# Dense passes of a four-layer graph network as one stream of steps, with layer 2 begun inside the graph norm

## The chip, the cores and the metric

The kernel runs on one core of a Trainium2 chip. TensorE (PE), VectorE (DVE), ScalarE (ACT) and GpSimd (POOL) each work through a queue of their own in order; SyncE (SP) issues most of the DMAs. Tensors live in HBM, tiles in SBUF, matmul results in PSUM. The metric is device time in microseconds (us); lower is better. A kernel is timed in several runs, and one further execution is profiled.

## What is computed

The graph has 6250 nodes with 128 features, and 206250 directed edges sorted by target. Four layers follow each other, each on `h = relu(layernorm(x))`. The reference, cut to what matters (edges as `src`, `dst`):

```python
# layer 0
nb = segment_sum(edge_weight[:, None] * h[src], dst)
x += leaky_relu(nb @ W1.T + b1 + (h * nb) @ W2.T + b2, 0.2)
# layer 1: mean over neighbours, then a norm over all nodes of the graph
f = gelu((segment_sum(h[src], dst) / max(deg, 1)) @ Wl.T + bl + h @ Wr.T)
out = f - mean_scale * mean(f)
x += out / sqrt(mean(out * out) + EPS) * gn_weight + gn_bias + h
# layer 2: nodes take the mean of clique rows
x += (segment_sum(x_clique[dst], src) / max(count, 1)) @ W.T + b
# layer 3: one message pass and a GRU cell
hh = h @ W_in.T + b_in
agg = segment_sum((hh @ W_msg)[src], dst)
r, z, n = gates(agg @ W_ih.T + b_ih, hh @ W_hh.T + b_hh)
x += ((1 - z) * n + z * hh) @ W_out.T + b_out
```

In layer 2, indices of `x_clique` (3125 rows) above the last one read the last row.

## The kernel before

Nodes are cut into 49 blocks of 128 (`NB`). A first stage, up to about 1225 us, counts for every pair of blocks how many edges lead from node to node. It writes the counts to HBM in bf16 as `cnt_d`, and a transposed copy as `cntT_d`, and does layer 0 on the way. With the counts, every later `segment_sum` is a dense product: the counts times the rows of the layer's input. Those are the three dense passes, each made by one call of the generator `dense` (L838 to L872), for layer 1 with `h_parts`, layer 2 with `q_parts` (the clique rows, 25 blocks, `NQB`) and layer 3 with `m_parts`.

`dense` goes over 13 chunks of up to four blocks of output nodes (`CHUNKS`; the seventh has one block). For each chunk it fills one PSUM accumulator `acc` (two buffers) in steps: seven steps of seven blocks for layers 1 and 3 (`by_node`), five steps of five blocks for layer 2. A step

- loads its rows of counts from `cnt_d` (L847, 896 KB) or `cntT_d` (L852, 640 KB) into a `ring` tile (three buffers), by SP's queue;
- turns them from bf16 into fp32r, some blocks on DVE into `some` (L858) and the others on ACT into `others` (L859), two buffers each; in layer 1 the same is done block by block with a sum taken along (L865, L868), which gives the degrees of layer 2;
- multiplies, two matmuls for each block (L870), since each input is kept as two halves whose sum is the fp32 value.

After a chunk's last step `dense` yields, and the caller works on that chunk.

- Layer 1 (from L943): copy `acc` to `agg`, a product with `wl`, scale and add, Gelu, and a sum over nodes on POOL. The first chunk is taken earlier, at L883 (`first = next(layer1)`); after it in the source stand the loads of `f` from `f_d` (L886), weights, the degrees (L902), and the clique rows `xq` (L914 to L918).
- The graph norm (L957 to L988): the mean from the sums (`over_all`, L938), then for each of 13 groups of four blocks a subtraction of `center` on DVE (L979), a square on ACT (L981) and a sum on POOL (L929, L932), then the `gain`.
- Layer 2 (from L993): copy of `acc` (L997), product with `wc` (L1001), load of `x` from `u_d` (L1004; tile `x` has two buffers), bias on POOL (L1005), `f` times gain and added to `x` (L1006, L1007), the chunk's update (L1009, L1012), the layer norm (helper `norm`, L554 to L565), the next bias on POOL (L1017), the store to `x_d` (L1018), and the input of layer 3 (L1021 to L1033: `hh`, `msg` and its halves in `m_parts`).
- Layer 3 (from L1036): the GRU gates, and the result.

No order is written out by hand. The framework that builds the program plans each engine's order itself: of the instructions whose inputs and buffers are ready at its planned time, it takes the one that stands first in the source. It then adds the waits. So a queue need not follow the source: the loads L1004 of layer 2's first two chunks are issued at 1199.9 us, in the counting stage, and matmuls of layer 2 run before layer 1's last product L950 at 1560.6 us. On the chip each queue is then worked through in the planned order, whether or not the times come out as planned.

Of the kernel before, what the change touches and what calls it, by code (L numbers as in the profile page):

```python
# [9 lines left out]
F32 = mybir.dt.float32  # L10
I32 = mybir.dt.int32
BF16 = mybir.dt.bfloat16
AF = mybir.ActivationFunctionType
ALU = mybir.AluOpType
DVE = mybir.EngineType.DVE

P = 128
D = 128
N = 6250
NB = -(-N // P)  # L20
# [453 lines left out]
CB = 4  # L474
NQB = -(-NQ // P)
CHUNKS = [(g, min(CB, n - g)) for b, n in ((0, NQB), (NQB, NB)) for g in range(b, n, CB)]
NCH = len(CHUNKS)
CHUNK_OF = {g + j: (c, j) for c, (g, nb) in enumerate(CHUNKS) for j in range(nb)}
KB = 7
KQ = 5  # L480
NSMP = -(-E // P)
F32R = mybir.dt.float32r
# [3 lines left out]
def fast(ctx: ExitStack, tc: tile.TileContext, a: dict, out: bass.AP, flag: bass.AP):  # L486


    nc = tc.nc
# [35 lines left out]
    cnt_d = dram.tile([NCH, P, CB, NB * P], BF16, name="cnt_d")  # L525
    cntT_d = dram.tile([P, NQB, NPAD], BF16, name="cntT_d")
# [54 lines left out]
    with ExitStack() as bx:  # L581
# [4 lines left out]
        psum = bx.enter_context(tc.tile_pool(name="b_psum", bufs=1, space=bass.MemoryType.PSUM))  # L586
# [250 lines left out]

    def dense(parts, by_node, seen=None):  # L838

        last, step, dve = (NB, KB, 4) if by_node else (NQB, KQ, 3)  # L840
        for c, (g, nb) in enumerate(CHUNKS):
            w = nb * P
            acc = psum.tile([P, CB * P], F32, name="acc", bufs=2)
            for q in range(0, last, step):
                if by_node:
                    t = ring.tile([P, CB, KB, P], BF16, name="ring")
                    nc.sync.dma_start(t[:, :nb].rearrange("p b k n -> p b (k n)"),  # L847
                                      cnt_d[c, :, :nb, q * P : (q + KB) * P])
                    t = t[:, :nb].rearrange("p b k n -> p k b n")
                else:  # L850
                    t = ring.tile([P, KQ, CB, P], BF16, name="ring")
                    nc.sync.dma_start(t[:, :, :nb].rearrange("p k b n -> p k (b n)"),  # L852
                                      cntT_d[:, q : q + KQ, g * P : g * P + w])
                    t = t[:, :, :nb]
                some = wide.tile([P, 4, CB, P], F32R, name="some")
                others = wide.tile([P, 3, CB, P], F32R, name="others")
                if seen is None:
                    nc.vector.tensor_copy(some[:, :dve, :nb], t[:, :dve])  # L858
                    nc.scalar.copy(others[:, : step - dve, :nb], t[:, dve:])  # L859
                for i in range(step):  # L860
                    rhs = some[:, i, :nb] if i < dve else others[:, i - dve, :nb]
                    if seen is not None:
                        total = seen[:, c, q + i : q + i + 1]
                        if i < dve:
                            nc.vector.tensor_scalar(rhs, t[:, i], 1.0, None, op0=ALU.mult,  # L865
                                                    op1=ALU.add, accum_out=total)
                        else:
                            nc.scalar.activation(rhs, t[:, i], AF.Copy, accum_out=total)  # L868
                    for j in range(2):
                        nc.tensor.matmul(acc[:, :w], parts[:, q + i, j, :], rhs,  # L870
                                         start=q + i + j == 0, stop=q + i + j == last)
            yield g, nb, acc  # L872


    h_parts = late.tile([P, NB, 2, D], F32R, name="parts")
# [4 lines left out]
        halves(nc.vector, [h_parts[:, g : g + nb, i, :] for i in range(2)], f[:, g : g + nb, :])  # L880
    deg2 = late.tile([P, NCH, NB], F32, name="deg2")
    layer1 = dense(h_parts, True, deg2)
    first = next(layer1)  # L883

    for g, nb in GROUPS:
        nc.sync.dma_start(f[:, g : g + nb, :], rows(f_d, g, nb))  # L886
# [22 lines left out]
    for g in range(0, NQB, GB):  # L909
        nb = min(GB, NQB - g)  # L910
# [14 lines left out]
    def over_nodes(total, blocks, g, nb):  # L925

        full = nb if g + nb < NB else nb - 1
        if full:
            nc.gpsimd.tensor_tensor(total[:, :full, :], total[:, :full, :], blocks[:, :full, :], op=ALU.add)  # L929
        if full < nb:  # L930
            last = total[:NR, full, :]
            nc.gpsimd.tensor_tensor(last, last, blocks[:NR, full, :], op=ALU.add)  # L932

    def over_all(total):

        p = psum.tile([P, D], F32, name="pS")
        for j in range(CB):
            nc.tensor.matmul(p, ones, total[:, j, :], start=j == 0, stop=j == CB - 1)  # L938
        return p

    f_sum = late.tile([P, CB, D], F32, name="f_sum")
    nc.gpsimd.memset(f_sum, 0.0)
    for g, nb, acc in chain((first,), layer1):  # L943
        w = nb * P
        agg = work.tile([P, CB * P], F32, name="wa")
        nc.scalar.copy(agg[:, :w], acc[:, :w])
        pa = psum.tile([P, CB * D], F32, name="pA")
        for j in range(nb):
            s = slice(j * D, (j + 1) * D)
            nc.tensor.matmul(pa[:, s], agg[:, s], wl, start=True, stop=True)  # L950
        for j in range(nb):
            nc.vector.scalar_tensor_tensor(f[:, g + j, :], pa[:, j * D : (j + 1) * D],
                                           inv1[:, g + j : g + j + 1], f[:, g + j, :],
                                           op0=ALU.mult, op1=ALU.add)
        fg = flat(f[:, g : g + nb, :])
        nc.scalar.activation(fg, fg, AF.Gelu)
        over_nodes(f_sum, f[:, g : g + nb, :], g, nb)  # L957
    p_sum = over_all(f_sum)
    center = late.tile([P, D], F32, name="center")
    nc.vector.scalar_tensor_tensor(center, p_sum, 1.0 / N, mean_scale, op0=ALU.mult, op1=ALU.mult)  # L960
# [12 lines left out]
    nc.vector.tensor_reduce(to_last, by_source[:, :, -(-NQB // CB) :], axis=mybir.AxisListType.X, op=ALU.add)  # L973
    nc.vector.tensor_mul(to_last, to_last, inv2)

    sq_sum = late.tile([P, CB, D], F32, name="f_sum")
    nc.gpsimd.memset(sq_sum, 0.0)
    for g, nb in GROUPS:
        nc.vector.tensor_sub(f[:, g : g + nb, :], f[:, g : g + nb, :], bcast(center, nb))  # L979
        sq = work.tile([P, GB, D], F32, name="wb")  # L980
        nc.scalar.activation(sq[:, :nb, :], f[:, g : g + nb, :], AF.Square)  # L981
        over_nodes(sq_sum, sq, g, nb)
    p_sq = over_all(sq_sum)
    gain = late.tile([P, D], F32, name="gain")
    nc.vector.tensor_scalar(gain, p_sq, 1.0 / N, EPS, op0=ALU.mult, op1=ALU.add)
# [3 lines left out]


    m_parts = late.tile([P, NB, 2, D], F32R, name="parts")
    hh = fh
    for g, nb, acc in dense(q_parts, False):  # L993
        w = nb * P
        cols = slice(g * P, g * P + w)
        agg = work.tile([P, CB * P], F32, name="wa")
        nc.scalar.copy(agg[:, :w], acc[:, :w])  # L997
        pa = psum.tile([P, CB * D], F32, name="pA")
        for j in range(nb):
            s = slice(j * D, (j + 1) * D)  # L1000
            nc.tensor.matmul(pa[:, s], agg[:, s], wc, start=True, stop=True)  # L1001
        x = work.tile([P, CB, D], F32, name="x")
        xg, fg = x[:, :nb, :], f[:, g : g + nb, :]
        nc.sync.dma_start(xg, rows(u_d, g, nb))  # L1004
        nc.gpsimd.tensor_tensor(xg, xg, bcast(b_res, nb), op=ALU.add)  # L1005
        nc.vector.tensor_mul(fg, fg, bcast(gain, nb))  # L1006
        nc.vector.tensor_add(xg, xg, fg)  # L1007
        for j in range(nb):
            nc.vector.scalar_tensor_tensor(x[:, j, :], pa[:, j * D : (j + 1) * D],  # L1009
                                           inv2[:, g + j : g + j + 1], x[:, j, :],  # L1010
                                           op0=ALU.mult, op1=ALU.add)
            nc.vector.scalar_tensor_tensor(x[:, j, :], last_out,  # L1012
                                           to_last[:, g + j : g + j + 1], x[:, j, :],
                                           op0=ALU.mult, op1=ALU.add)
        h = work.tile([P, CB, D], F32, name="wb")
        norm(xg, h, nb)
        nc.gpsimd.tensor_tensor(xg, xg, bcast(b_out, nb), op=ALU.add)  # L1017
        nc.sync.dma_start(rows(x_d, g, nb), xg)  # L1018
        pt = psum.tile([P, CB * P], F32, name="pT")
        for j in range(nb):  # L1020
            nc.tensor.transpose(pt[:, j * P : (j + 1) * P], h[:, j, :], ident)  # L1021
        ht = work.tile([P, CB * P], F32, name="wc")
        nc.scalar.copy(ht[:, :w], pt[:, :w])
        ph = psum.tile([P, CB * P], F32, name="pB")
        nc.tensor.matmul(ph[:, :w], w_in, ht[:, :w], start=True, stop=True)
        nc.scalar.activation(hh[:, cols], ph[:, :w], AF.Identity, bias=b_in)
        pm = psum.tile([P, CB * D], F32, name="pT")
        for j in range(nb):
            nc.tensor.matmul(pm[:, j * D : (j + 1) * D], hh[:, (g + j) * P : (g + j + 1) * P],
                             w_msg, start=True, stop=True)  # L1030
        msg = work.tile([P, CB, D], F32, name="wd")
        nc.scalar.copy(flat(msg[:, :nb, :]), pm[:, :w])
        halves(nc.vector, [m_parts[:, g : g + nb, i, :] for i in range(2)], msg[:, :nb, :])  # L1033


    for g, nb, acc in dense(m_parts, True):  # L1036
        w = nb * P
        cols = slice(g * P, g * P + w)
        agg = work.tile([P, CB * P], F32, name="wa")
# [97 lines left out]
```

## Time and profile before

| | |
|---|---|
| median of three runs | 2179.38 us (2178.58 to 2182.17) |
| profiled execution | 2177.09 us |
| its span in the trace | 2175.3 us |
| mean granted TensorE clock | 0.962 of full speed |
| busy: PE, PE weight loads, DVE, ACT, POOL | 88%, 72%, 65%, 54%, 16% of the span |
| DMA | 406.32 MB, mean 187 GB/s |
| matmuls L870, all three passes | 3198, busy 836.9 us in their four groups of the page |

A profile row of a group gives line, engine, operation, the tile written and the tiles read, the shape and the count. Then come the busy time, the mean of one in ns, and the engine's idle time just before these instructions with what ended it. In a timeline each row has its start and length in us, and square brackets hold the idle time before it and what ended that. A table by windows gives the busy time of each engine in stretches of the span. The chain of waits goes back from the last instruction, at each step to what released it. "SPq" is SP's queue, which only issues DMAs.

### The profile page before, as it was taken

The numbers are of one execution on the slowest core, as the hardware profiler recorded it, in microseconds if no ns is written. First come the engines' busy times: TensorE is split into PE (matmuls) and PEld (weight loads), VectorE is DVE, ScalarE is ACT, GpSimd is POOL, SyncE is SP. The second block draws the span as 40 slices with busy tenths as digits, with TensorE's granted clock in tenths as the row PEclk, the third lists the DMA queues.
The fourth block names the chain that finished last, engine by engine and source line by source line (L and its number), as shares of the span: only waits on it lengthen the run. The fifth ranks groups of instructions, "written<-read, shape, count | busy, mean of one in ns | idle before, by whom it ended". The sixth has DMA issues, their size and how long they took to land. (4 is left out here: it accounts for less than half of the span.)

```text
span 2175.3 us, 60376 instructions
## 1 busy us (share of the span) xinstructions
PE 1910.5 (88%) x25624; PEld 1564.8 (72%) x25624; DVE 1411.9 (65%) x3349; ACT 1174.2 (54%) x2692; POOL 348.3 (16%) x377
## 2 busy tenths in 40 slices
PE   0579988889898999998999679999878899999998
PEld 0557777777787888777888558878756667777775
DVE  6887767767676776776775458677776554443443
ACT  1745656555555666566666146566545555443443
POOL 4531211222212122111100020000231110000000
PEclk9989999999999999999999789999989999999999
DMA  2579999999998222223122698688755778776773
GB/s 63 154 177 229 216 213 212 231 204 217 220 229 194 86 105 93 90 85 105 73 101 103 197 265 278 214 283 270 228 164 174 231 236 262 239 229 197 237 239 128
DMA packets 423787, 406.32 MB, mean 187 GB/s; under 512 B 191216, under 2 KB 414307, under 8 KB 417235
## 3 DMA queue, kind: packets, MB, share of 16 engines
q1 hardware_dynamic: 414883, 394.35, 64.1%
q0 software_dynamic: 5600, 6.56, 1.3%
q8 instruction: 203, 3.33, 0.6%
q10 hardware_dynamic: 3024, 1.45, 0.3%
q14 instruction: 77, 0.63, 0.1%
HBM read 227.26 MB, written 134.89 MB: 166 GB/s over the span
## 5 line engine op out<-in xcount | busy, mean ns | idle before, releaser
L727 ACT CAST cnt<-pK 128x392 bf16<-128x392 f32 x784 | 407.5, 520 | 342.1 <-PE pK L713 289.5
L749 PE MATMUL pL<-edge_w,h 128*128 128x256 f32 (+1 forms) x2450 | 590.0, 392 | 1.1 <-issue 0.8
L713 PE MATMUL pK<-k_hot,s_hot 64*128 64x49 bf16 (+1 forms) x18816 | 420.8, 195 | 126.4 <-ACT edge_w L728 66.0
L713 PEld LDWEIGHTS <-s_hot 64*128 64x128 bf16 x18816 | 371.0, 96 | 197.2 <-issue 119.8
L749 PEld LDWEIGHTS pL<-edge_w,h 128*128 128x128 f32 x2450 | 456.9, 196 | 66.2 <-issue 1.2
L728 ACT COPY edge_w<-pK 128x392 f32<-128x392 f32 x784 | 415.1, 529 | 0.0
L870 PE MATMUL acc<-some,parts 128*128 128x512 f32 (+1 forms) x1456 | 369.4, 395 | 31.3 <-DVE some L865 20.6
L870 PEld LDWEIGHTS acc<-some,parts 128*128 128x128 f32 x1456 | 269.6, 192 | 95.7 <-DVE some L865 24.4
L696 DVE TENSOR_TENSOR s_hot<-iota,by_edge 128x2048 bf16<-128x2048 bf16 x196 | 239.3, 1221 | 133.7 <-PE pK L713 129.2
L700 DVE TENSOR_TENSOR k_hot<-k_hot,by_edge 128x784 bf16<-128x784 bf16 x588 | 307.9, 576 | 5.2
L859 ACT CAST others<-ring 128x1536 fp32r<-128x1536 bf16 (+3 forms) x156 | 192.4, 1233 | 198.3 <-PE acc L870 132.2
L858 DVE CAST some<-ring 128x2048 fp32r<-128x2048 bf16 (+3 forms) x156 | 165.7, 1063 | 177.8 <-PE acc L870 151.6
L870 PE MATMUL acc<-others,parts 128*128 128x512 f32 (+1 forms) x1092 | 277.7, 388 | 0.0
L865 DVE TENSOR_SCALAR_CACHE_REDUCE some<-ring 128x512 fp32r<-128x512 bf16 (+1 forms) x364 | 216.6, 651 | 62.7 <-PE acc L870 43.1
L870 PEld LDWEIGHTS acc<-others,parts 128*128 128x128 f32 x1092 | 202.5, 191 | 42.5 <-issue 0.5
L868 ACT ACTIVATE others<-ring 128x512 fp32r<-128x512 bf16 (+1 forms) x273 | 162.3, 597 | 113.1 <-issue 59.6
L870 PE MATMUL acc<-some,q_parts 128*128 128x512 f32 (+1 forms) x390 | 111.5, 412 | 30.6 <-DVE some L858 30.6
L698 DVE TENSOR_TENSOR k_hot<-iota,by_edge 128x784 bf16<-128x784 bf16 x196 | 114.4, 583 | 0.0
L870 PEld LDWEIGHTS acc<-some,q_parts 128*128 128x128 f32 x390 | 71.2, 196 | 51.4 <-DVE some L858 35.5
L657 DVE TENSOR_SCALAR_CACHE_REDUCE same<-dst,node 128x64 bf16<-128x64 int32 x50 | 13.9, 277 | 137.7 <-DMA dst<-in_dst,off_i 137.7
L780 POOL TENSOR_TENSOR xs<-xs,h 128x256 f32<-128x256 f32 (+1 forms) x25 | 27.3, 1090 | 466.3 <-ACT h L565 466.3
L870 PE MATMUL acc<-others,q_parts 128*128 128x512 f32 (+1 forms) x260 | 78.3, 409 | 0.0
(155 smaller groups left out, 1520.6 us busy)
## 6 DMA issues: line engine op xcount, KB each, us to landing
ring<-cnt_d SPq DMA_DIRECT2D x168, 896.0 KB
cnt_d<-cnt SPq DMA_DIRECT2D x49, 1568.0 KB
cntT_d<-tt SPq DMA_DIRECT2D x175, 224.0 KB
ring<-cntT_d SPq DMA_DIRECT2D x60, 640.0 KB
ring<-cnt_d SPq DMA_DIRECT2D x14, 224.0 KB
xs<-in_x SPq DMA_DIRECT2D x24, 128.0 KB
xs<-in_x SPq DMA_DIRECT2D x12, 256.0 KB
h_d<-h SPq DMA_DIRECT2D x24, 128.0 KB
```

What stands on the lines that cost most here:

```text
L696: nc.vector.tensor_tensor(s_hot, count_up(P), at(0, P), op=ALU.is_equal)
L698: nc.vector.tensor_tensor(k_hot[:, 0], count_up(NB), at(1, NB), op=ALU.is_equal)
L700: nc.vector.tensor_tensor(k_hot[:, i], k_hot[:, 0], at(1 + i, NB), op=ALU.mult)
L713: nc.tensor.matmul(pk[:, h, to], s_hot[r, u, :, t], rhs, start=j == 0, stop=True, skip_group_check=True)
L727: nc.scalar.copy(to_nodes(mats[n0 // P][:, :, n0 % P : n0 % P + nn]), by_block(0))
L728: nc.scalar.copy(to_nodes(edge_w[:, :, n0 : n0 + nn]), by_block(1))
L749: nc.tensor.matmul(pl[:, :w], h0[:, s, :], edge_w[:, s, :w], start=s == 0, stop=s == NB - 1)
L858: nc.vector.tensor_copy(some[:, :dve, :nb], t[:, :dve])
L859: nc.scalar.copy(others[:, : step - dve, :nb], t[:, dve:])
L865: nc.vector.tensor_scalar(rhs, t[:, i], 1.0, None, op0=ALU.mult, op1=ALU.add, accum_out=total)
L868: nc.scalar.activation(rhs, t[:, i], AF.Copy, accum_out=total)
L870: nc.tensor.matmul(acc[:, :w], parts[:, q + i, j, :], rhs, start=q + i + j == 0, stop=q + i + j == last)
```

## The change

`dense` becomes a stream over all steps of all chunks. A new inner function `bring` holds what a step did before its matmuls: the load, and both casts. The stream brings the next step, then issues the matmuls of the current one. The next step of a chunk's last step is the first step of the next chunk, so that one now stands in the source ahead of the work on the finished chunk. `dense` also yields `None` before each step; `chunks` leaves these out for callers that want whole chunks.

Layer 2's stream is made right after layer 1's last chunk, and its first step is brought there, ahead of `over_all`. In the graph norm's loop, one `next(layer2)` follows each group's subtraction, square and sum, until two chunks are complete; they are kept in `ahead`. Layer 3's first step is brought before the work on layer 2's last chunk. At the start of layer 1, the first step of the second chunk now stands ahead of the loads L886.

The number of loads, casts and matmuls, their shapes, and the buffers stay as they were.

```diff
+        def bring(c, g, nb, q):
...
+            some = wide.tile([P, 4, CB, P], F32R, name="some")
+            others = wide.tile([P, 3, CB, P], F32R, name="others")
+            if seen is None:
+                nc.vector.tensor_copy(some[:, :dve, :nb], t[:, :dve])
+                nc.scalar.copy(others[:, : step - dve, :nb], t[:, dve:])
...
+            return rhs
+
+        steps = [(c, g, nb, q) for c, (g, nb) in enumerate(CHUNKS) for q in range(0, last, step)]
+        ready = bring(*steps[0])
+        for n, (c, g, nb, q) in enumerate(steps):
+            yield
+            now = ready
+            if n + 1 < len(steps):
+                ready = bring(*steps[n + 1])
+            if q == 0:
+                acc = psum.tile([P, CB * P], F32, name="acc", bufs=2)
+            for i in range(step):
+                for j in range(2):
+                    nc.tensor.matmul(acc[:, : nb * P], parts[:, q + i, j, :], now[i],
+                                     start=q + i + j == 0, stop=q + i + j == last)
+            if q + step == last:
+                yield g, nb, acc
+
+    def chunks(layer):
+        return (c for c in layer if c is not None)
...
-    first = next(layer1)
+    first = next(chunks(layer1))
...
-    for g, nb, acc in chain((first,), layer1):
+    for g, nb, acc in chain((first,), chunks(layer1)):
...
+    layer2 = dense(q_parts, False)
+    next(layer2)
     p_sum = over_all(f_sum)
...
+    ahead = []
     for g, nb in GROUPS:
...
         over_nodes(sq_sum, sq, g, nb)
+        if len(ahead) < 2:
+            ahead.append(next(layer2))
+            ahead = [c for c in ahead if c is not None]
...
+    layer3 = dense(m_parts, True)
-    for g, nb, acc in dense(q_parts, False):
+    for g, nb, acc in chain(ahead, chunks(layer2)):
...
+        if g + nb == NB:
+            next(layer3)
...
-    for g, nb, acc in dense(m_parts, True):
+    for g, nb, acc in chunks(layer3):
```

More of the change, by code (lines that the diff above doesn't have):

```diff
@@ L840, in dense @@
         last, step, dve = (NB, KB, 4) if by_node else (NQB, KQ, 3)
[L841 to L849, printed above, removed]
-                else:
[L851 to L872, printed above, removed]
@@ new lines, in bring @@
+        def bring(c, g, nb, q):
+            if by_node:
+                t = ring.tile([P, CB, KB, P], BF16, name="ring")
+                nc.sync.dma_start(t[:, :nb].rearrange("p b k n -> p b (k n)"),
+                                  cnt_d[c, :, :nb, q * P : (q + KB) * P])
+                t = t[:, :nb].rearrange("p b k n -> p k b n")
+            else:
+                t = ring.tile([P, KQ, CB, P], BF16, name="ring")
+                nc.sync.dma_start(t[:, :, :nb].rearrange("p k b n -> p k (b n)"),
+                                  cntT_d[:, q : q + KQ, g * P : (g + nb) * P])
+                t = t[:, :, :nb]
+            some = wide.tile([P, 4, CB, P], F32R, name="some")
[3 more added lines that the diff above has]
+                nc.scalar.copy(others[:, : step - dve, :nb], t[:, dve:])
+            rhs = [some[:, i, :nb] if i < dve else others[:, i - dve, :nb] for i in range(step)]
+            for i in range(step if seen is not None else 0):
+                total = seen[:, c, q + i : q + i + 1]
+                if i < dve:
+                    nc.vector.tensor_scalar(rhs[i], t[:, i], 1.0, None, op0=ALU.mult,
+                                            op1=ALU.add, accum_out=total)
+                else:
+                    nc.scalar.activation(rhs[i], t[:, i], AF.Copy, accum_out=total)
+            return rhs
```

## The prediction

> **What bounds the kernel now.** I read the page's busy shares first (PE 88% of the span), then the table by windows, cut where the work changes. Its columns are the stretch, its length, busy time of PE, PE's weight loads, DVE, ACT, POOL with counts, then granted clock, DMA share, GB/s.
>
> ```profile
> 1225.00:1281.00 56.00, 29.37 (x107) 22.72 (x106) 33.74 (x93) 16.53 (x46) 11.59 (x12) 0.71 0.98 258
> 1281.00:1566.00 285.00, 281.31 (x1286) 229.76 (x1286) 217.14 (x726) 172.71 (x532) 18.98 (x18) 0.98 0.84 264
> 1566.00:1597.00 31.00, 14.35 (x63) 11.52 (x64) 24.31 (x20) 13.61 (x21) 21.57 (x16) 0.72 0.28 83
> 1597.00:1788.00 191.00, 170.86 (x803) 130.48 (x802) 119.48 (x323) 98.29 (x157) 30.21 (x22) 0.97 0.70 209
> 1788.00:1973.00 185.00, 184.16 (x769) 136.07 (x767) 81.61 (x103) 86.34 (x85) 2.61 (x2) 1.00 0.73 233
> ```
>
> All before 1225 us is the counting stage, which the change doesn't touch. Layer 1 (to 1566) and layer 3 (from 1788) keep PE over 98% busy: a border there has nothing to give. PE is idle in three places: the fill of layer 1 (26.6 us of 56, at a DMA share of 0.98), the graph norm (16.7 of 31), and layer 2 (20.1 of 191).
>
> The timelines of PE, DVE and POOL (start, length, engine, line, operation, count, idle time before and what ended it) show the norm:
>
> ```profile
> 1571.36 1.10 PE L870 MATMUL acc<-others,q_parts 128*128 128x512 f32 x4
> 1587.18 2.08 PE L870 MATMUL acc<-some,q_parts 128*128 128x512 f32 x4 [14.72 <-DVE some L858]
> 1590.78 2.07 PE L938 MATMUL pS<-f_sum,f_ones 128*128 128x128 f32 x8 [1.52 <-POOL f_sum L932]
> ...
> 1568.01 18.25 DVE L979 TENSOR_TENSOR fh<-fh,center 128x512 f32<-128x512 f32 x13
> 1586.17 2.89 DVE L858 CAST some<-ring 128x1536 fp32r<-128x1536 bf16 x2
> ...
> 1569.51 20.68 POOL L929 TENSOR_TENSOR f_sum<-f_sum,wb 128x512 f32<-128x512 f32 x12 [1.35 <-ACT wb L981]
> ```
>
> Layer 2's first four steps have already run when the norm begins: the order on an engine is the planner's, not the source's. Then all 13 subtractions stand on DVE ahead of the cast for step 4, and PE waits 14.72 us, restarting slowly (four matmuls in 2.08 us against 0.94 elsewhere). POOL's sums end the norm at 1590.7; the gain follows at 1597.3 and the first update at 1599.8.
>
> Layer 2's idle time comes from the chain of waits; its columns are start, length and what:
>
> ```profile
> 1721.11 1.31 POOL x L1017
> 1722.43 2.75 DMA x_d<-x
> 1725.25 3.30 DMA x<-u_d
> 1728.67 1.29 POOL x L1005
> 1729.98 0.69 DVE x L1007
> ```
>
> The issues counted in order give the names: x_d<-x here is chunk 7, x<-u_d is chunk 9 (tile x has two buffers), and L1007 of chunk 9 stands on DVE **ahead of chunk 8's updates** L1009 to L1012. So update, norm, L1017, write, read, L1005, L1007, next update is a ring of 16.94 us a chunk (L1007 at 1729.98, then at 1746.92). PE waits 1.75 us for a cast in most chunks. The ring, not PE, paces layer 2.
>
> **Layer 1's fill.** SP's order is: steps 3 to 6, thirteen loads fh<-f_d (1254.3 to 1267.0), inv, last_row and loads of xq, then step 7 at 1274.3. The change issues step 7 ahead of f_d, so every load behind it in SP's queue moves back by 896 KB (3.5 us at the window's 258 GB/s). PE can run step 7 at about 1267 instead of 1281.2. But step 8 still comes behind f_d, inv and some of xq; the bytes through step 11 are the same, and DMA is full. If step 8 takes step 7's old place, it reaches DVE near 1280.5 + 3.5 = 1284, against 1286.6 now, and then runs after a pause; step 7's first matmuls after its pause took 3.78 + 2.37 us where 3.2 is usual. 2.6 us earlier less 2.9 of slow start, of which one step's slack hides about half: I take **-1.2 us**, ends 0 and -3.
>
> **Borders.** The casts, loads and matmuls are the same in number and size, with the same three ring and two wide buffers, so how far a load can run ahead is unchanged. In layer 2 the next chunk's first two casts already stand ahead of the updates (1722.26 and 1726.71, updates from 1730.59). Putting the first of them there in the source too: **0**. In layer 3 the one real hole is 3.20 us, after the one-block chunk, and ends with a DMA of 896 KB; no buffer is added, so **0**, ends -3 and +3. The first step of layer 3 ahead of layer 2's last update also gains nothing: PE is already full there. A cast moved there costs DVE 1.23 us, hidden by that full PE; uncovered, it costs that once.
>
> **Layer 2 in the norm.** Steps may now come between groups: the cast of step i+1 stands after group i's subtraction, so steps 4 to 9 may go in among subtractions 3 to 10. A cast also needs the matmuls two steps back; PE takes 2.33 us a step (1597.78 to 1600.11) and a subtraction 1.40 on average, so between 3 and 7 casts find room. I take **5**, the middle. PE gains 5 x 2.33 + 1.1 for the slow restart = 12.8 us of lead. The steps' loads find a DMA share of 0.28 in that window. Both accumulators may be full by then; chunk 2's matmuls need only chunk 0's copy L997, which waits for no gain. ACT's casts (1.05 us) and squares (0.63) sit in waits that ACT has now (1.04 us after each square); if uncovered, 5 us.
>
> The price is on the norm's own path. One rule of the Trainium skill speaks against this edit: "SBUF — State Buffer", section "Who interferes with whom". DVE and GpSimd share a port pair as an exclusive lock, taken by a DVE cast in its two-port mode or by a DVE instruction with two SBUF inputs, and the loser waits out the other's whole instruction. The rows: a subtraction takes 0.682 us before POOL starts and 1.745 (median) beside it; of the two casts at the end, one took 0.947 and the other 2.026 beside a POOL sum. By the rule each cast waits out a sum: 0.96 + 1.29 (a POOL pass alone, L1005) = 2.25, five of them 11.2. By the two rows the mean is 1.49, so 7.4. The last subtraction ends at 1586.2 and its square starts at 1588.3, so 2.1 of that is covered. The gain comes 9.1 us later by the rule, 5.3 by the rows; I take **5.3**, ends 0 (three casts, all beside idle POOL) and 9.
>
> What is late next? The first update goes from 1599.8 to 1605.1. From there the ring decides: first update to third, through x_d<-x of chunk 0 and x<-u_d of chunk 2. From the first update to L1007 of chunk 2 took 21.7 us at the start (one L1017 took 3.82), the steady ring 16.9; between them 19.3. The third update then starts near 1625.1, against 1632.4 now, where it waited for PE (L1001 at 1631.0, which with the lead is at 1618). So 12.8 us of lead become **7.3**; after that 16.9 a chunk, as now.
>
> **Sum:** 7.3 + 1.2 = 8.5 off the profiled execution's 2177.1 (span 2175.3 and 1.8 around it), so 2168.6. Runs shown have a median 2.3 above that execution; I forecast against the median: 2179.4 - 8.5 = **2171**. This case spans 2164 (norm not delayed, fill -3) to 2177 (norm nine late, 21.7 in the first round). A difference under 0.2% (4.4 us) can't be told from none.
>
> **Rivals.**
>
> The ring breaks. With PE ahead, an update may be ready when its own x is, and the planner then need not put the next chunk's L1007 ahead of it. Two buffers would let the ring take 8.5 us a chunk and PE would pace layer 2. All 12.8 of lead stay, two thirds of the 20.1 us of waits go (13.4), and the fill's 1.2: 2179.4 - 27.4 = 2152. For it: the waits at casts are short and regular. Against: steady layer 2 is planned from unchanged parts, and once the updates catch up, L1007 is ready first again.
>
> The planner doesn't do it. Subtractions are ready at once and casts wait for PE; if it still puts 11 or more first, the gap stays: 2179, within 4.
>
> Slower: the ring lengthens. If the step brought ahead puts one more ring<-cntT_d issue between x_d<-x and x<-u_d in SP's queue, the read waits for 640 KB, 3.1 us at 209 GB/s. Over eight rounds that is +25, less 8.5: 2196. It decides above 1.1 us a chunk. For it: one such issue stands there already, and x<-u_d took 2.72 to 3.84 us. Against: that cast's ring slot comes free at the same time as now.
>
> **Chances.** Forecast 0.55, broken ring 0.27, no effect 0.11, longer ring 0.07. The range must hold the first and most of the second: 2148 to 2179; outside it lie the longer ring and the tails. The forecast gives faster 0.8 of its chance, same the rest; the broken ring is all faster: 0.44 + 0.27 + a little = 0.74 faster, 0.18 same, 0.08 slower.
>
> **What would show it.** After: some casts L858 among the L979 rows; PE's wait of 14.72 split into waits of 2 to 4 us; the first L1009 some 5 us later, counted from the first L979; the third some 7 earlier; L1007 still waiting for L1005 and 16.9 us between them; step 7 ahead of fh<-f_d. I am wrong if layer 2's PE waits of 1.75 us are gone (then 2152), if L979 still runs 13 in a row, or if x<-u_d lands later.

## The result, and the profile after

| | before | after |
|---|---|---|
| median | 2179.5 us (2176.0 to 2187.7, 12 runs) | 2177.1 us (2164.0 to 2183.0, 12 runs) |
| ratio, 95% interval | | 0.9979 (0.9961 to 0.9997) |
| profiled execution, its span | 2177.1, 2175.3 us | 2178.6, 2176.8 us |

By the ratio the change gains 0.2%, some 4.5 us, and the two medians lie 2.4 us apart; 8.4 were forecast. The profiled execution of after is even 1.5 us longer than that of before. The table by windows of the changed kernel, from the norm on, shows that PE's idle time moved. Columns as before: stretch, length, busy time and count of PE, weight loads, DVE, ACT, POOL, then clock, DMA share, GB/s.

```profile
1566.00:1601.00 35.00, 27.80 (x122) 21.70 (x123) 29.96 (x27) 19.18 (x28) 22.60 (x15) 0.95 0.62 180
1601.00:1788.00 187.00, 164.46 (x743) 125.78 (x742) 118.40 (x316) 91.76 (x149) 30.44 (x22) 0.92 0.65 193
```

In the norm PE works 27.8 of 35 us now, where it worked 14.4 of 31. In layer 2 it is idle for 22.5 of 187 us, where it was idle for 20.1 of 191.

The timelines of DVE and PE in the changed kernel's norm show why:

```profile
1567.44 3.59 DVE L996 TENSOR_TENSOR fh<-fh,center 128x512 f32<-128x512 f32 x4
1570.95 2.04 DVE L857 CAST some<-ring 128x1536 fp32r<-128x1536 bf16 x1
1572.91 1.77 DVE L996 TENSOR_TENSOR fh<-fh,center 128x512 f32<-128x512 f32 x1
1574.60 2.05 DVE L857 CAST some<-ring 128x1536 fp32r<-128x1536 bf16 x1
1576.57 2.38 DVE L996 TENSOR_TENSOR fh<-fh,center 128x512 f32<-128x512 f32 x2
1578.87 0.95 DVE L857 CAST some<-ring 128x1536 fp32r<-128x1536 bf16 x1
...
1573.04 1.66 PE L880 MATMUL acc<-some,q_parts 128*128 128x512 f32 x6 [1.16 <-DVE some L857]
...
1586.87 2.88 PE L880 MATMUL acc<-some,q_parts 128*128 128x512 f32 x6 [4.40 <-DVE some L857]
```

Five casts stand among the 13 subtractions: the three above and two at 1584.8 and 1589.0. PE's one wait of 14.72 us has become four, of 0.57 to 4.40.

Where did the lead go? I count layer 2's steps from 0, by the order of casts and matmuls. The matmuls of step 12 start 34.5 us after the first subtraction, 15.2 sooner than in before (49.7). Those of step 13 start at 44.6, only 7.5 sooner (52.1). DVE works without a pause between the casts for these two steps, mostly on the updates and norms of the first two chunks:

```profile
1599.77 0.90 DVE L857 CAST some<-ring 128x1536 fp32r<-128x1536 bf16 x1
...
1609.72 0.93 DVE L857 CAST some<-ring 128x1536 fp32r<-128x1536 bf16 x1
...
1612.05 2.52 PE L880 MATMUL acc<-some,q_parts 128*128 128x512 f32 x4
...
1622.20 1.06 PE L1024 MATMUL pA<-f_WcT,wa 128*128 128x128 f32 x8
```

So the product of chunk 2 (L1024, the last line) starts 54.8 us after the first subtraction, 8.2 sooner than in before. A later stretch of the changed kernel's DVE timeline stands ahead of the third update (L1032):

```profile
1620.94 0.68 DVE L1030 TENSOR_TENSOR x<-x,fh 128x512 f32<-128x512 f32 x1
1621.54 0.95 DVE L857 CAST some<-ring 128x1536 fp32r<-128x1536 bf16 x1
1622.41 3.09 DVE L1029 TENSOR_TENSOR fh<-fh,gain 128x512 f32<-128x512 f32 x5
1625.42 0.41 DVE L577 CAST parts<-wd 128x512 fp32r<-128x512 f32 x1
1625.76 0.34 DVE L1032 SCALAR_TENSOR_TENSOR x<-pA,inv,x 128x128 f32<-128x128 f32 x1
```

Its `x` is ready at 1621.6 and its product at 1623.3, but five multiplications by the gain for later chunks stand in front of the update. And in the chain of waits of the changed kernel (start, length, what) one round of the ring reads:

```profile
1718.51 2.28 DMA x_d<-x
...
1720.85 5.38 DMA x<-u_d
...
1727.68 0.69 DVE x L1030
```

It is the same ring, but the read took 5.38 us where it took 3.30 before. The four rounds from the eighth to the twelfth update took 17.6 to 18.5 us instead of 16.9 to 17.0; they eat the lead that the norm made. Whether the change does that, or one execution, is for the experiments.

For them I cut each profile into stages (lengths in us, from the timelines; updates are counted by chunks; a negative length means that the update no longer waits for the gain; the last column runs from the last product, L1067 in before and L1090 in after, of the chunk before the one-block chunk to that of the one-block chunk). The kernels are those of the experiments below.

| kernel | first matmul to first subtraction | to gain's product | to first update | to third update | to 13th update | layer 3's one-block chunk |
|---|---|---|---|---|---|---|
| before | 335.4 | 29.0 | 2.7 | 32.6 | 164.6 | 21.8 |
| before_again | 331.5 | 30.1 | 2.7 | 30.9 | 172.0 | 21.0 |
| borders_only | 334.8 | 30.0 | 2.7 | 31.1 | 165.9 | 27.4 |
| after | 333.8 | 33.1 | 2.7 | 22.4 | 171.3 | 21.3 |
| after_again | 330.5 | 33.8 | 2.7 | 22.8 | 165.6 | 20.7 |
| norm_only | 333.1 | 33.0 | 2.7 | 22.2 | 164.5 | 21.6 |
| x3_after | 331.5 | 33.6 | 2.7 | 22.7 | 163.3 | 27.4 |
| dve_only | 331.8 | 28.6 | 2.7 | 20.1 | 164.9 | 21.4 |
| addlast_before | 334.2 | 29.9 | 0.2 | 29.0 | 158.2 | 25.8 |
| addlast_after | 336.6 | 32.5 | -2.4 | 25.3 | 154.4 | 27.4 |
| dve_sum | 332.8 | 26.9 | -6.7 | 28.9 | 154.3 | 21.2 |
| fill | 318.2 | 32.4 | -2.4 | 25.3 | 155.2 | 22.0 |
| fill_dve | 318.5 | 26.8 | -6.7 | 28.7 | 154.6 | 25.8 |

The first matmul of layer 1 itself starts between 1232.6 and 1242.1 us in these profiles, in code that none of the kernels changes. So stages are compared, not times from the span's start.

### The profile page after: what moved, and what is told of

It is laid out like the page before. It is cut to its first block, busy times and chain, and to the rows that moved or that the text cites. A ratio compares the mean times of both kernels' runs of the same rounds, so it can differ in the third digit from the quotient of the medians.

```text
span 2176.8 us, 60377 instructions
## 1 busy us (share of the span) xinstructions
PE 1916.5 (88%) x25624; PEld 1569.7 (72%) x25624; DVE 1415.8 (65%) x3349; ACT 1174.3 (54%) x2692; POOL 350.4 (16%) x377
## 3 DMA queue, kind: packets, MB, share of 16 engines
q1 hardware_dynamic: 414883, 394.35, 64.3%
## 5 line engine op out<-in xcount | busy, mean ns | idle before, releaser
L880 PE MATMUL acc<-some,q_parts 128*128 128x512 f32 (+1 forms) x390 | 116.3, 427 | 25.4 <-DVE some L857 25.4
```

The source lines that it names most:

```text
L880: nc.tensor.matmul(acc[:, : nb * P], parts[:, q + i, j, :], now[i], start=q + i + j == 0, stop=q + i + j == last)
```

## The experiments

Ratios are against the kernel before, timed in turn with each kernel on the same chip; its median there was 2184.9, 2186.3 and 2177.4 us in three sets.

### Which part gains: the norm alone, the borders alone

norm_only makes layers 1 and 3 by the old generator and keeps only layer 2's start in the norm:

```diff
-    layer1 = dense(h_parts, True, deg2)
-    first = next(chunks(layer1))
+    layer1 = dense_old(h_parts, True, deg2)
+    first = next(layer1)
...
-        if g + nb == NB:
-            next(layer3)
...
-    for g, nb, acc in chunks(layer3):
+    for g, nb, acc in dense_old(m_parts, True):
```

> Only layer 2 is a stream and begins inside the norm; layers 1 and 3 are as before. If borders and layer starts are worth nothing (my sum: 0 and 1.2 for the fill): 2172 to 2179, within 2 us of the changed kernel. If the stream over borders matters: more than 3 us away from the changed kernel.

borders_only keeps the streams and takes the steps out of the norm's loop:

```diff
-        if len(ahead) < 2:
-            ahead.append(next(layer2))
-            ahead = [c for c in ahead if c is not None]
```

> The changed kernel without the steps taken in the norm's loop: the stream over borders and layer 2's first step ahead of the norm stay, no next(layer2) follows a group. My theory (all of the gain is made in the norm, the borders and the fill are worth 0 to 1.6 us): PE's wait of about 14.7 us in the norm is back, first subtraction to third update is back at 63 to 65 us (before 64.3, after 58.2), and the time is that of the kernel before within 3 us, ratio 0.9985 to 1.0015. Rival 1 (borders make the gain): first subtraction to third update is still 64, but the ratio is 0.998 or below and the gain lies in layer 1 or 3. Rival 2 (borders cost what the norm gains, which would explain why the changed kernel gains so little in the times): ratio 1.002 or above.

norm_only: 2182.9 us, ratio 0.9990 (0.9974 to 1.0006). borders_only: 2186.4 us, ratio 1.0004 (0.9986 to 1.0022). By the times each is equal to the kernel before, so they alone can't divide a gain this small. The medians of norm_only and after_again, run side by side, lie 3.3 us apart, which my expectation had put down to the borders; their ratios (0.9990 and 0.9993) don't differ. The stages decide. From first subtraction to third update norm_only takes 57.9 us, as after does (58.2), and borders_only 63.8, as before does (64.3). The timeline of borders_only has the old wait back to the hundredth:

```profile
1593.86 2.08 PE L880 MATMUL acc<-some,q_parts 128*128 128x512 f32 x4 [14.72 <-DVE some L857]
```

What the stages show of the change comes from the steps in the norm.

### How much of it is the execution: both kernels again

> The changed kernel once more, for a second profile. Theory A (the ring of waits in layer 2 gives the lead back because the read x<-u_d lands later in the rounds from chunk 7 on, by chance of the transfers, the queues being in the same order in both kernels): the third update comes 6 to 7 us earlier than in the kernel before, as in the first profile, but the rounds 7 to 11 need not be 17.7 us again; the gain at the last update lies anywhere from 0 to 8 us, and the time is 2170 to 2179. Theory B (the longer rounds are a fixed effect of the change): rounds 7 to 11 are again 17.6 to 18.5 us, the last update comes no earlier than before, and the time is 2177 to 2180.

> The kernel before, unchanged, against itself: what a ratio and its interval are worth here, and a second profile of the ring. Ratio 0.998 to 1.002. If rounds of the ring over 17.5 us (four of five late rounds in the first profile of the changed kernel) come from how long transfers take in one execution, such rounds appear here too, or the mean round lies between 16.7 and 17.3; if they belong to the change, all eight rounds from third to eleventh interval are 16.8 to 17.1.

after_again: 2179.6 us, ratio 0.9993 (0.9974 to 1.0012). before_again: 2178.8 us, ratio 1.0009 (0.9993 to 1.0025): the kernel before against itself. The second profile of before has the long rounds of the ring that I had seen in after; its chain of waits, with L1007 at 1729.67:

```profile
1720.02 2.25 DMA x_d<-x
...
1722.34 5.88 DMA x<-u_d
```

The same four rounds took 19.0, 18.7, 16.7 and 18.1 us here, and this execution needed 172.0 us from third to 13th update. after_again needed 165.6. So the given-back lead of the first profile of after doesn't belong to the change: x<-u_d takes 2.7 to 5.9 us from one round to the next in the two profiles of before, and 2.8 to 5.4 in the two of after. In three of these four rounds write and read took 8.1, 5.8 and 7.3 us together and the whole round 10.9 us more each time: the ring passes such a delay on in full. The other long round (18.7) isn't on that chain; there the chain runs over PE and the halves of layer 3's input (L578).

### The ring: order or buffers

addlast_before and addlast_after move one line of layer 2 behind the updates, in the old and in the changed kernel. The sum is added in another order, nothing else differs:

```diff
-        nc.vector.tensor_add(xg, xg, fg)
         for j in range(nb):
...
+        nc.vector.tensor_add(xg, xg, fg)
         h = work.tile([P, CB, D], F32, name="wb")
```

> The kernel before with the same move of the addition. Ring theory: the 1.75 us a chunk go, some 12 to 17 us in all: 2162 to 2168; and against it the changed kernel with the move is 8 to 13 us faster, which is the lead that the norm gives (12.8 less what the norm's end is late, as PE then paces). Rival: 2176 to 2180, and the two kernels with the move are as far apart as those without, 2 to 5 us.

> The changed kernel with the addition x + f of layer 2 put behind the chunk's updates, so that the next chunk's addition can no longer stand ahead of them on DVE. Ring theory: PE paces layer 2, the lead of the norm is kept and most of layer 2's 20 us of PE waits go: 2150 to 2160, updates about 15 us apart. Rival (layer 2 is paced by DVE's work or by the DMAs, and the ring only looks like the bound): 2172 to 2179, updates still about 17 us apart.

x3_after gives tile `x` of layer 2 a third buffer and leaves the line where it was. Layer 3's tile of the same name gets one too:

```diff
-        x = work.tile([P, CB, D], F32, name="x")
+        x = work.tile([P, CB, D], F32, name="x", bufs=3)
...
-        x = work.tile([P, CB, D], F32, name="x")
+        x = work.tile([P, CB, D], F32, name="x", bufs=3)
```

> The changed kernel with three x buffers in layer 2 in place of two. The addition now stands two chunks ahead of the updates, so the ring is closed again, one buffer further on. My theory: updates stay 16.5 to 17.5 us apart and the time is that of the changed kernel, ratio 0.996 to 1.001. Rival (the ring is a lack of buffers, not of order): a third buffer lets PE pace layer 2, updates 14 to 15.5 us apart, ratio 0.991 to 0.994.

addlast_before: 2173.4 us, 0.9945 (0.9921 to 0.9969). addlast_after: 2168.3 us, 0.9927 (0.9903 to 0.9950). x3_after: 2173.7 us, 0.9981 (0.9961 to 1.0001), as the changed kernel itself. addlast_before gains some 12 us, the least that I had expected, and addlast_after some 16 where I had 19 to 29. The updates of x3_after stay 15.2 to 16.8 us apart from the fourth to the twelfth, somewhat closer than my 16.5 to 17.5, but from third to 13th update it needs 163.3 us, about as much as norm_only with two buffers (164.5). Counting L1030 and L1032 in DVE's order gives the reason: in the changed kernel, as in before, the addition of chunk 8 stands ahead of chunk 7's updates; in x3_after it stands ahead of chunk 6's; in addlast_after behind its own chunk's. So what closes the ring is that L1007 (L1030 after) of a later chunk stands ahead of an update in DVE's queue, which works in order, and a third buffer lets the planner put it there earlier still. The waits of PE in layer 2, of before, of after and of addlast_after (who waited for whom, us in total, times, longest):

```profile
PE acc L870 <- DVE some L858: 14.7, 10, 1.9
PE pT L1021 <- ACT wb L565: 3.8, 3, 1.9
```

```profile
PE acc L880 <- DVE some L857: 18.2, 9, 4.0
PE pT L1044 <- ACT wb L565: 2.7, 2, 2.5
```

```profile
PE pT L1044 <- ACT wb L565: 7.2, 5, 2.8
PE acc L880 <- DVE some L857: 3.4, 4, 1.0
```

With the ring open the lead from the norm is kept: from first subtraction to 13th update addlast_before takes 217.3 us and addlast_after 209.8, so 7.5 less. I had expected 8 to 13. The medians differ by 5.1 us, though the intervals of the two ratios overlap.

### What the casts cost the norm

dve_only is the changed kernel with the norm's sums of squares on DVE in place of POOL (the mean's sums stay on POOL). DVE, the busier engine, gets 13 instructions more:

```diff
-    def over_nodes(total, blocks, g, nb):
+    def over_nodes(total, blocks, g, nb, eng=None):
...
-            nc.gpsimd.tensor_tensor(total[:, :full, :], total[:, :full, :], blocks[:, :full, :], op=ALU.add)
+            (eng or nc.gpsimd).tensor_tensor(total[:, :full, :], total[:, :full, :], blocks[:, :full, :], op=ALU.add)
...
-        over_nodes(sq_sum, sq, g, nb)
+        over_nodes(sq_sum, sq, g, nb, nc.vector)
```

> The changed kernel with one edit: the norm's sums of squares on DVE in place of POOL; layer 2's addition stays ahead of the updates, so the ring stays. This prices the forecast's term 'gain and first update late by 5.3 us'. Lock theory: subtractions 0.68, casts 0.95, first subtraction to gain 26 to 28 us (33.1 in the changed kernel), the casts no longer delay the norm; first subtraction to third update 51 to 54 us (58.2), since the ring starts from the first update, and the time falls by 4 to 7 us, ratio 0.994 to 0.997. Rival (in the ring every lead is eaten by layer 2, as the first profile of the changed kernel seemed to show): first subtraction to 13th update stays at 225 to 230 us, ratio 0.998 to 1.000.

dve_sum is the same edit on addlast_after.

> The changed kernel with two edits: layer 2's addition behind the updates (as in addlast_after), and the norm's sums of squares on DVE in place of POOL. If the slow subtractions and casts in the norm come from POOL's sums on the same port (subtraction 0.68 us alone, 1.75 beside a sum; cast 0.95 and 2.05), subtractions and casts return to 0.68 and 0.95, a sum on DVE takes 0.7 to 1.1 us, and first subtraction to gain goes from 33 to 25 to 29 us: 3 to 7 us less than addlast_after (0.9927), ratio 0.989 to 0.992. Rival (no interference; DVE simply has 12 instructions more): DVE's stretch in the norm grows by 12 to 16 us, first subtraction to gain is 34 us or more, ratio 0.993 or above.

dve_only: 2161.1 us, 0.9929 (0.9902 to 0.9955). dve_sum: 2157.1 us, 0.9872 (0.9840 to 0.9903). Both gain more than expected. The timeline of dve_only's norm:

```profile
1574.57 0.69 DVE L996 TENSOR_TENSOR fh<-fh,center 128x512 f32<-128x512 f32 x1
1575.17 0.69 DVE L943 TENSOR_TENSOR f_sum<-f_sum,wb 128x512 f32<-128x512 f32 x1
1575.77 0.95 DVE L857 CAST some<-ring 128x1536 fp32r<-128x1536 bf16 x1
1576.64 0.69 DVE L943 TENSOR_TENSOR f_sum<-f_sum,wb 128x512 f32<-128x512 f32 x1
```

With no sum on POOL beside them every subtraction of four blocks takes about 0.7 us (1.75 in the median before), every cast up to the last subtraction 0.95 or 0.96 (up to 2.05 in after), and a sum 0.7. The changed kernel shows the same within one run, in its POOL timeline:

```profile
1568.94 8.86 POOL L943 TENSOR_TENSOR f_sum<-f_sum,wb 128x512 f32<-128x512 f32 x5 [1.34 <-ACT wb L998]
1579.21 8.73 POOL L943 TENSOR_TENSOR f_sum<-f_sum,wb 128x512 f32<-128x512 f32 x5 [1.42 <-ACT wb L998]
1589.36 3.93 POOL L943 TENSOR_TENSOR f_sum<-f_sum,wb 128x512 f32<-128x512 f32 x2 [1.42 <-ACT wb L998]
```

The two casts of 0.95 us (1578.87 and 1589.02) start in POOL's pauses, the three of 2.02 to 2.05 while a sum runs. DVE does its work up to the last subtraction in 20.2 us, with eleven sums and seven casts in between, where the changed kernel takes 23.8 with five casts and no sum. First subtraction to gain takes 28.6 us against 33.1. Not all of that need be the slow DVE instructions: the same edit takes the sums off POOL, where before they ended the norm, and no run has the sums on DVE without the casts. A cast that waited 1.12 us for its load still stands ahead of the gain's last product. From first subtraction to 13th update dve_only takes 216.3 us, 12.6 less than before, so the ring doesn't eat every lead; that rival falls.

### Layer 1's fill

In the changed kernel PE runs step 7 early and then waits for step 8, whose load stands behind 13 loads of f, inv, and some of xq in SP's queue. PE's wait before step 8 and SP's queue in the changed kernel:

```profile
1284.01 3.78 PE L880 MATMUL acc<-some,parts 128*128 128x512 f32 x8 [12.99 <-DVE some L863]
1287.59 2.65 PE L880 MATMUL acc<-others,parts 128*128 128x512 f32 x6
...
1258.42 11.71 SPq L900 DMA_DIRECT2D fh<-f_d  x13
...
1270.71 6.64 SPq L930 DMA_DIRECT2D xq<-in_x_clique  x2
```

fill starts from addlast_after and loads each chunk's rows of `f` in that chunk's turn of layer 1's loop; the block of the clique rows (`q_parts`, `xq`, `last_row`) moves behind that loop. fill_dve adds the edit of dve_sum.

```diff
-    for g, nb in GROUPS:
-        nc.sync.dma_start(f[:, g : g + nb, :], rows(f_d, g, nb))
...
     for g, nb, acc in chain((first,), chunks(layer1)):
+        nc.sync.dma_start(f[:, g : g + nb, :], rows(f_d, g, nb))
...
+    q_parts = late.tile([P, NQB, 2, D], F32R, name="q_parts")
...
     layer2 = dense(q_parts, False)
```

> The changed kernel with the addition behind the updates, and layer 1's first steps freed of what is not needed there: each chunk's rows of f are loaded in its own turn of layer 1's loop, and the clique rows (xq, last_row and their halves) stand behind layer 1. If the fill's idle time of PE (12.99 us before step 8, and a slow restart of some 3 us) comes from these loads ahead of step 8 in SP's queue, that wait falls below 4 us and the first matmul to first subtraction shrinks from 333 to 337 by 8 to 14 us: ratio 0.987 to 0.989 against addlast_after's 0.9927. Rival (DMA is full in the fill anyway, the same bytes come sooner or later and PE meets the wait at another step): 0 to -3 us, ratio 0.991 to 0.993.

> Both edits of dve_sum and fill together. If both theories hold and the two gains lie in stages that do not touch each other, they add: ratio the product of dve_sum's and fill's over addlast_after's, about 0.983 to 0.988, the fastest of all kernels here. If layer 2 then meets another limit (the clique rows come late, PE waits there), it is no better than fill alone.

fill: 2149.7 us, 0.9844 (0.9814 to 0.9875). Its timeline at the same step:

```profile
1275.32 2.56 PE L880 MATMUL acc<-some,parts 128*128 128x512 f32 x8 [1.73 <-DVE some L863]
1277.71 1.56 PE L880 MATMUL acc<-others,parts 128*128 128x512 f32 x6
```

The wait is 1.73 us, the restart takes 2.56 + 1.56 us instead of 3.78 + 2.65, and layer 1 takes 318.2 us instead of 330.5 to 336.6 in the kernels with the old loads. That is 12 to 18 us less where I had 8 to 14, and the ratio is lower than the expected 0.987 to 0.989. DMA was full there, but with bytes that weren't needed yet. The edit moves the rows of `f` and the clique rows together; which of them counts more wasn't tried. fill_dve: 2146.6 us, 0.9810 (0.9775 to 0.9845), the lowest median of all kernels here. The product of the single gains would be 0.979; its interval overlaps fill's, so that the two add is likely and not shown by the times. Its stages show both: 318.5 in the first column as in fill, 26.8 in the second as in dve_sum.

## Why the prediction was right in kind and too large in size

The forecast of 2171 us stands against 2177.1; the range (2148 to 2179) holds it. The ratios 0.9979 and 0.9993 of the two sets are gains of 4.5 and 1.5 us, at the bound of what can be told or under it. By the time alone the rival "the planner doesn't do it" (2179, within 4) fits better than the forecast; only the profiles rule it out. That the range held is luck in part: its end is 1.9 us away, and the two sets differ by 3 us.

- **Casts in the norm**: five forecast, five found. The 14.72 us wait broke up, into four of 0.57 to 4.40 where I had 2 to 4.
- **Norm late by 5.3**: right in kind. First subtraction to gain took 33.0 to 33.8 us in after, after_again, norm_only and x3_after, 29.0 to 30.1 in before, before_again and borders_only: 3.7 later in the mean (33.4 less 29.7). The rule's price of one cast (2.25) is near the 2.02 to 2.05 of the three casts that met a sum; charging it to all five (9.1) was too much, since two started in POOL's pauses. That DVE instructions last longer beside POOL's sums, as the Trainium skill ("SBUF — State Buffer", section "Who interferes with whom") has it for a DVE instruction with two SBUF inputs, dve_only shows: without the sums a subtraction takes 0.69 us in place of 1.75. What share of the 3.7 us that makes is open.
- **First to third update**: this term failed. I let the ring decide and took 20.0 us, by way of 19.3 to L1007 of chunk 2 and its steady distance of 0.7 to the update. The stage took 22.2 to 22.8 us. L1030 came sooner (17.6 after the first update in after), but the update 4.8 later, for two reasons. Its product started 54.8 us after the first subtraction, where I had 50.2 (63.0 less 12.8): PE's lead had reached 15.2 us, but the cast for step 13 stood on DVE behind the first two chunks' updates and norms. Then the cast, five L1029 and L577 stood between L1030 and the update. In before such products (L1006) ran at 1623.1 while the third update waited for PE; with PE early, their cover was gone. x3_after bears this out: there L1030 of chunk 2 starts 12.0 us ahead of the update, and the stage still takes 22.7. I asked what is late next among the links of the ring, and not what else DVE's queue holds ahead of the casts and the update.
- **Lead of 7.3**: first subtraction to third update is 63.9 us in the mean of before, before_again and borders_only, 58.6 in that of after, after_again, norm_only and x3_after: **5.3**. First to third update gave 9.0 (31.5 less 22.5 in the means) where I had 12.6, partly since my one profile of before had the longest such stage; the norm took 3.7 of it where I had 5.3.
- **"After that 16.9 a chunk, as now"**: right in the mean, wrong for one execution. 164.6, 172.0 and 165.9 us without steps in the norm, 171.3, 165.6, 164.5 and 163.3 with them. One profile of before gave me a round that looked constant to a few hundredths.
- **Fill -1.2**: step 7 ran early and step 8 at 1284.0, after a pause and with a slow restart, as worked out. The net lies within the scatter of that stage (331.5 to 335.4 with the old stream, 330.5 to 336.6 with the new and the loads where they were).
- **Borders 0**: right; borders_only 1.0004.
- **Broken ring, 2152**: didn't happen, because the planner still put L1030 first. Opened by hand it was worth 0.9945 in the kernel before and 0.9927 in the changed one: about 16 us where I had 27.4 for it. PE then waits 7.2 us for ACT's wb (3.8 in before), which I had not counted.
- **Longer ring, 2196**: from the third update to the last the five engines' queues hold the same order in both kernels, and long reads occur in before too.

What stays open is the distance from the 5.3 us seen in the stages to the 1.5 to 4.5 in the ratios: it is inside the intervals, and no run tells it from the scatter.

## What to carry to other kernels

Work that fills an idle engine pays only as far as the next in-order queue lets it: list everything that stands in that queue ahead of the instruction that should come earlier, also what was hidden until now. Where one transfer a round paces a loop, look for the line that makes it a ring, and move the line before adding buffers; here one moved addition did more than the whole change. And a DMA that is full is no bound until one has asked whether its bytes are needed there.

## What the hardware did that I had not expected

The granted TensorE clock halved for some 20 us after a wait of PE of 1.40 us. All 13 profiles have that wait in layer 3, ahead of the last product of the chunk before the one-block chunk. In eight the clock stayed at 1.00 until a second wait of 2.5 to 3.2 us some 14 us later. In five (borders_only, x3_after, addlast_before, addlast_after, fill_dve) it fell at once. Timeline and windows of addlast_after:

```profile
1959.17 1.49 PE L1090 MATMUL pA<-f_W_outT,wd 128*128 128x128 f32 x8 [1.40 <-DVE wd L1086]
1960.79 1.91 PE L880 MATMUL acc<-some,parts 128*128 128x128 f32 x8
```

```profile
1960.00:1965.00 5.00, 5.00 (x26) 5.00 (x25) 1.11 (x2) 1.02 (x2) 0.00 (x0) 0.50 0.40 111
...
1975.00:1980.00 5.00, 5.00 (x24) 4.90 (x24) 2.13 (x2) 2.53 (x3) 0.00 (x0) 0.50 0.74 218
```

Eight such matmuls took 1.91 us, where before took 1.06 at the same place. The stage then lasted 25.8 to 27.4 us instead of 20.7 to 22.0, so one execution can be about 4 to 7 us longer than the next by this alone, as much as the change is worth. The wait alone doesn't decide it, as all 13 have it; what does wasn't tried.

The second surprise is the price of two engines side by side: moving 13 sums from POOL to the busier DVE made DVE's own work in the norm shorter, by 3.6 us up to the last subtraction.
